# One weight product in the head of a convolution-and-attention kernel, by Strassen's rule

## Chip, cores and metric

The kernel runs on one NeuronCore of a Trainium2 chip. Times are device microseconds of one execution. Inputs and outputs are float32.

## What is computed

The reference has two layers. The first is an attention with deformed keys: a grouped 1x1 projection gives q, a depthwise convolution of q gives offsets, the input is sampled at the offset places, and a small network of positions (2 to 128 to 128 to 1) gives a bias for each of 1024 queries and 64 keys of each group. Softmax, output projection, and an MLP of 512 to 2048 to 512 follow. The second layer is a self-attention over the 1024 positions of each of two images. Cut to what matters:

```
bias = jax.nn.relu(bias @ cpb_w1 + cpb_b1)
bias = jax.nn.relu(bias @ cpb_w2 + cpb_b2)
bias = (bias @ cpb_w3 + cpb_b3).reshape(b, GROUPS, H * W, Hd * Wd)
sim = jnp.einsum('bhid,bhjd->bhij', qh, kh) + bias
...
q = xt @ Wq.T + bq
k = xt @ Wk.T + bk
v = xt @ Wv.T + bv
attn = jax.nn.softmax(jnp.einsum('bnc,bmc->bnm', q, k) / jnp.sqrt(jnp.float32(c)), axis=-1)
out = jnp.einsum('bnm,bmc->bnc', attn, v)
out = out @ Wp.T + bp
```

The kernel multiplies the weights of the second layer with each other beforehand: one 512x512 product joins Wq with Wk, and a second one joins Wv with Wp. The second product is the subject here.

## The kernel before

The work has four stages that follow each other.

*The head* (about the first 37 us). The offset chain of the first group runs: `chain(0)` projects q (L285), sums 36 taps of the depthwise convolution on VectorE (one L321 or L323 operation each, the two inputs being q in `qa` and the running sum `acc`), applies gelu on ScalarE (L355), multiplies on TensorE (L367), takes tanh (L377), and computes the positional values `fe` on VectorE and ScalarE by turns (L390 to L417). They are written to the DRAM tensor `fdr` (L418) and read back as `fb`, spread over all partitions (L599). From `fb`, ScalarE and VectorE make the tables `ta` and `tb` (L610, L616). Meanwhile `rank`, `order` and `arrange` sort the channels of the bias network by sign. They use small GpSimd operations (L233 to L235, and L260 to L266 for the scales `sc` and the small matrices `w3f` and `w3u`). TensorE fills its time with the two weight products `weights(0)` and `weights(1)`.

A weight product takes 16 matmuls of 128x128 weights by 512 columns into two PSUM tiles (L549), two ScalarE copies of 128x1024 into a half of the tile `gs` (L555), and one store to DRAM, `gdr[i]`, from GpSimd's queue (L557). `weights(1)` reads `wls[1]`, loaded by two transfers of 1 MB on the queue of SyncE (L537). The second layer reads both stored products back much later (`load_g`).

*The bias loop* (256 steps, most of the time). For each step s, `st_layer1` makes a tile `h1` of 128x4096 from `ta` and `tb` by one custom VectorE operation (L630; step 0 does it in two halves of 128x2048). `st_layer2` multiplies it in four parts z of eight matmuls (L647), each part into one of three PSUM tiles of the pool `zp`; ScalarE evicts each part (L656, L658), and VectorE adds them in pairs (L666, `st_sum`). Up to three `h1` tiles exist, in buffers of the tag `h1` that the two `wl_s` tiles and `gs` also use in the head. Steps 0 and 1 have small extra matmuls (`psu`, L515) behind them. Adding up the lanes of the sums is done by transfers.

*The projection and MLP*, and *the self-attention*, already use Strassen's rule for their large products. Its helpers stand at the top of the kernel:

```
PARTS = {1: (0, 0), 2: (1, 2), 3: (6, 3), 4: (2, 6), 5: (4, 4), 6: (5, 5), 7: (3, 1)}
FOLD = ((4, 3, 2), (5, 4, 0), (6, 5, 1), (3, 3, 0))
def fold(engine, w, sign=ALU.add, which=range(4)):
    for i in which:
        o, u, v = FOLD[i]
        engine.tensor_tensor(w[o], w[u], w[v], ALU.add if i % 2 else sign)
```

`fold` makes the four sums of one operand's blocks, `spread` (L125, L128) those of the other, always on VectorE. `PARTS` tells which block of each operand enters which of the seven products. `plus` (L137) is a VectorE sum.

Nothing sets the order of the work but the program: each engine runs its instructions in the order in which they are issued, which follows the program and a scheduler's estimate; `tc.issue_after(x)` gives an instruction a place behind x. The head's pieces are generators that are advanced by hand:

```
with tc.issue_after(newest(PE)):
    next(n)
for _ in n:
    pass
```

where `n` is the second product. Here its matmuls come behind those of `arrange` on TensorE.

Of the kernel before, what the change touches and what calls it, by code (L numbers as in the profile page):

```python
# [8 lines left out]
F32 = mybir.dt.float32  # L9
AF = mybir.ActivationFunctionType  # L10
ALU = mybir.AluOpType
# [3 lines left out]
P = 128  # L15
# [42 lines left out]
def conv_seq_kernel(ctx: ExitStack, tc: tile.TileContext, x, xt, kst, pst, cst, vec, wsm, outw, w1, w2, wl, wlt, brow, out):  # L58
    nc = tc.nc
# [4 lines left out]
    def newest(engine):  # L64
        return next(i for i in reversed(nc.cur_bb.bb.instructions) if i.engine == engine)
# [26 lines left out]
    gdr = [dp.tile([P, NCH, C], F32, name=f"gdr{i}") for i in range(2)]  # L92
    ub = cp.tile([P, 2, NCH], F32, name="ub")
# [18 lines left out]
    PARTS = {1: (0, 0), 2: (1, 2), 3: (6, 3), 4: (2, 6), 5: (4, 4), 6: (5, 5), 7: (3, 1)}  # L112
# [3 lines left out]
# [5 lines that stand above are left out]
    def spread(x, which=range(4)):  # L121
        for i in which:
            if i % 2 == 0:
                o, u = ((4, 0), (1, 3))[i // 2]
                nc.vector.tensor_tensor(x[o], x[u], x[1], ALU.subtract)  # L125
            else:
                o, u, v = ((5, 4, 3), (6, 5, 2))[i // 2]
                nc.vector.scalar_tensor_tensor(x[o], x[u], -1.0, x[v], ALU.mult, ALU.subtract)  # L128
# [7 lines left out]
    def plus(out, a, b_, op=ALU.add):  # L136
        nc.vector.tensor_tensor(out, a, b_, op)  # L137
# [8 lines left out]
    zp = ctx.enter_context(tc.tile_pool(name="zp", bufs=3, space=PSUM))  # L146
# [9 lines left out]
    with tc.tile_pool(name="lp", bufs=2) as lp:  # L156
# [80 lines left out]
        def order():  # L237
            nc.vector.tensor_scalar(k8, eight, rn[:, 1:2], 8.0, ALU.is_le, ALU.mult)
            nc.vector.tensor_reduce(t8, k8, AX.X, ALU.add)
            free, bound = ([t.rearrange("p (a b l) -> p b a l", a=2, b=2)[:, i] for t in (place, crow)] for i in (0, 1))  # L240
            nc.vector.tensor_scalar(bound[0], bound[1], t8, 64.0, ALU.is_ge, ALU.mult)
            nc.vector.tensor_tensor(bound[0], bound[0], bound[1], ALU.add)
            nc.vector.tensor_scalar(free[0], free[1], t8, None, ALU.add)
            nc.vector.tensor_scalar(perm, place, pc, None, ALU.is_equal)
# [26 lines left out]
        def chain(ci):  # L271
# [3 lines left out]
            for i in range(K):  # L275
                k = k0 + i
# [5 lines left out]
                ps = flat("psq")  # L282
# [76 lines left out]
            if ci == 0:  # L359
                ps = [simp.tile([P, 512], F32, name="sim") for _ in range(2)]  # L360
            else:
                ps = flat("po").rearrange("p (f m) -> p f m", f=2)
                ps = [ps[:, f] for f in range(2)]
# [24 lines left out]
            def place_keys(i0, i1):  # L388
                for i in range(i0, i1):
                    nc.vector.scalar_tensor_tensor(  # L390
                        th[:, i], th[:, i], 4.0, jg[:, i].unsqueeze(1).to_broadcast([P, 2 * K, J]),
                        ALU.mult, ALU.add,
                    )
                t = thf[:, i0 * n : i1 * n]
                nc.vector.tensor_scalar(t, t, 2.0 / 7.0, -1.0, ALU.mult, ALU.add)
# [4 lines left out]
            pos, ab, u, ln, er = (fe[0:64, i, :] for i in range(5))  # L400
# [5 lines left out]
            if ci > 0:  # L406
# [12 lines left out]
                out=fdr[ci].rearrange("g c p j -> p (g c) j"), in_=ab.rearrange("p (g j) -> p g j", j=KT)  # L419
            )  # L420
            if ci == 0:
                place_keys(0, 2)
            state[ci] = th
            yield
# [107 lines left out]
        wls = [lp.tile([P, 2, NCH, C], F32, tag="h1", name="wl_s", bufs=3) for _ in range(2)]  # L532
# [8 lines left out]
        gs = lp.tile([P, 2, NCH, C], F32, tag="h1", name="gs", bufs=3)  # L541

        def weights(i):
            ps = [flat("psg") for _ in range(2)]
            for o in range(NCH):
                for k in range(NCH):
                    if i == 0 and (o, k) in ((1, 0), (3, 1)):
                        yield
                    nc.tensor.matmul(  # L549
                        ps[k // 2][:, k % 2 * 512 : k % 2 * 512 + 512], wls[i][:, 0, o, k * P : (k + 1) * P],  # L550
                        wls[i][:, 1, o, :], start=(o == 0), stop=(o == NCH - 1),
                    )
            yield
            for k2 in range(2):
                nc.scalar.copy(gs[:, i, 2 * k2 : 2 * k2 + 2, :].rearrange("p k o -> p (k o)"), ps[k2])  # L555
            yield
            nc.gpsimd.dma_start(out=gdr[i], in_=gs[:, i])  # L557


        PE = mybir.EngineType.PE  # L560
        marks = []
        head, g, n = chain(0), weights(0), weights(1)
        next(head)
        next(g)
        with tc.issue_after(newest(PE)):
# [6 lines left out]
        with tc.issue_after(newest(PE)):  # L572
            next(g)
        order()
        for _ in head:
            pass
        with tc.issue_after(newest(mybir.EngineType.Activation)):
            next(g)
        with tc.issue_after(newest(PE)):
# [216 lines left out]
        for s in range(NS):  # L796
# [36 lines left out]
            if bg is None and s > ready and (s - ready) % 4 == 0 and (s - ready) // 4 <= 8:  # L833
                i = (s - ready) // 4 - 1
# [32 lines left out]
    uc = xq.tile([P, 2], F32, name="uc")  # L867
# [16 lines left out]
    with ExitStack() as top, tc.tile_pool(name="wp", bufs=2) as wp:  # L884
# [14 lines left out]
        for i, (b, h) in enumerate(halves):  # L899
            for o in range(NCH):  # L900
                n = slice(h * 512, (h + 1) * 512)
# [157 lines left out]
        for i, (b, p) in enumerate(units):  # L1059

            j, k = divmod(i, NCH)
# [324 lines left out]
```

## Time and profile before

| what | us |
|---|---|
| median of three runs | 2642.21 (2642.19 to 2644.27) |
| the profiled execution | 2641.35 |
| its span, first to last instruction | 2639.6 |
| TensorE busy | 2627.4 |
| VectorE busy | 2244.4 |
| ScalarE busy | 1693.6 |
| GpSimd busy | 783.6 |

The profile is that of one execution. A matmul of float32 stands in it as two records, so the 16 matmuls of a product are 32 records. PE is TensorE, PEld its weight loads, DVE VectorE, ACT ScalarE, POOL GpSimd, SP SyncE; L549 is line 549 of the kernel. A timeline row has its start and its length in us, the engine, the line, the operation, output and inputs, and in brackets how long the engine had been idle and what released it. In a view of groups, `| busy, mean ns | idle before` are totals and the mean of one. The shares of busy time are averages over the four stages; a change in the head is read from the head. The rows of the DMA view for the time from 26 to 28 us, and for that from 32 to 36 us, give each issue's size and the time to its landing:

```profile
gdr<-gs POOLq DMA_DIRECT2D x1, 1024.0 KB, 5.7
fb<-fdr SPq DMA_DIRECT2D x1, 512.0 KB, 5.7
```

```profile
fb<-fdr SPq DMA_DIRECT2D x1, 512.0 KB, 3.7
```

### The profile page before, as it was taken

How to read it: one execution, taken by the hardware profiler on the slowest of the kernel's cores; microseconds unless marked ns; L12 is line 12 of the kernel's file. 1: busy time of each engine (PE TensorE's matmuls, PEld its weight loads, DVE VectorE, ACT ScalarE, POOL GpSimd, SP SyncE). 2: the span in 40 equal slices, each digit the busy share in tenths (PEclk: the TensorE clock that was granted, in tenths of full speed). 3: DMA queues.
4: the chain of work that ended last, by engine and by line, in shares of the span. 5: the costliest groups of instructions: out<-in, count | busy, mean ns of one | idle time of the engine just before them, and what ended most of it. 6: DMA issues, size and time to landing. Idle time of an engine off the chain costs nothing.

```text
span 2639.6 us, 46955 instructions
## 1 busy us (share of the span) xinstructions
PE 2627.4 (100%) x19368; PEld 959.2 (36%) x19368; DVE 2244.4 (85%) x1333; ACT 1693.6 (64%) x2222; POOL 783.6 (30%) x863
## 2 busy tenths in 40 slices
PE   9999999999999999999999999999999999999999
PEld 3333322333333233333333333333344444446454
DVE  7999999999999999999999999999674494466354
ACT  5887898888888878887887777777621131114041
POOL 1333333333333333333333333333332232000000
PEclk9999999999999999999999999999999999999999
DMA  5788877888878888888887878788721111000000
GB/s 189 178 178 173 197 165 167 183 181 196 174 170 172 182 181 191 178 175 174 174 181 171 176 173 181 173 176 180 190 87 50 42 56 56 4 17 0 32 1 32
DMA packets 116294, 366.77 MB, mean 139 GB/s; under 512 B 23376, under 2 KB 27616, under 8 KB 113392
## 3 DMA queue, kind: packets, MB, share of 16 engines
q0 software_dynamic: 69408, 235.31, 47.5%
q1 hardware_dynamic: 46240, 128.15, 13.6%
q8 instruction: 153, 2.51, 0.4%
q14 instruction: 61, 0.50, 0.1%
q10 hardware_dynamic: 432, 0.31, 0.0%
HBM read 74.81 MB, written 6.55 MB: 31 GB/s over the span
## 4 chain that ended last, share of the span: by engine, by line
PE 93%; DVE 2%; ACT 2%; issue 2%; DMA 0%; DVEq 0%; ACTq 0%
PE ps L647 61%; PE sw L966 15%; PE sw L1101 9%; PE sw L913 2%; PE sw L1199 2%; PE sim L733 1%; DVE h L630 1%; PE psg L549 1%; ACT rx L656 0%; DVE ub L666 0%; ACT ub L658 0%; ACT prod L331 0%; PE pkv L483 0%; PE sim L716 0%; PE pt L750 0%
## 5 line engine op out<-in xcount | busy, mean ns | idle before, releaser
L647 PE MATMUL ps<-h,cw 128*32 128x512 f32 x16384 | 1777.2, 592 | 5.0 <-ACT rx L656 3.9
L630 DVE CUSTOM_DVE_ANT_1 h<-ta,tb 128x4096 f32<-128x4096 f32 (+1 forms) x257 | 1131.0, 4402 | 28.8 <-PE ps L647 25.8
L647 PEld LDWEIGHTS ps<-h,cw 128*32 128x32 f32 x16384 | 548.4, 110 | 1197.4 <-issue 1124.5
L656 ACT ACTIVATE rx<-ps,sc 128x1024 f32<-128x1024 f32 x512 | 567.8, 1109 | 145.7 <-PE ps L647 127.7
L658 ACT ACTIVATE ub<-ps,sc 128x1024 f32<-128x1024 f32 x256 | 308.0, 1203 | 93.7 <-PE ps L647 93.6
L666 DVE SCALAR_TENSOR_TENSOR ub<-rx,sc,ub 128x1024 f32<-128x1024 f32 x256 | 326.9, 1277 | 6.6 <-ACT ub L658 6.6
L685 POOL DMA_DIRECT2D ua<-uc x126 | 158.0, 1271 | 308.9 <-DMA ua<-uc 298.9
L685 POOL DMA_DIRECT2D ua<-ua x189 | 224.7, 1360 | 18.4 <-DMA ua<-uo 14.3
L966 PE MATMUL sw<-hm,w2t 128*128 128x512 f32 x448 | 193.6, 592 | 0.0
L966 PE MATMUL sw<-xb,w1t 128*128 128x512 f32 x448 | 193.6, 592 | 0.0
L668 POOL DMA_DIRECT2D uo<-ub x127 | 125.9, 991 | 222.7 <-DVE ub L666 207.0
L658 ACT ACTIVATE uo<-ps,sc 128x1024 f32<-128x1024 f32 x128 | 154.1, 1204 | 53.1 <-PE ps L647 52.7
L666 DVE SCALAR_TENSOR_TENSOR uo<-rx,sc,uo 128x1024 f32<-128x1024 f32 x128 | 163.6, 1278 | 9.4 <-ACT uo L658 9.2
L137 DVE TENSOR_TENSOR hm<-hm,sw 128x1024 f32<-128x1024 f32 x56 | 67.5, 1218 | 105.7 <-PE sw L966 105.5
L685 POOL DMA_DIRECT2D uc<-uo x63 | 53.6, 852 | 323.8 <-DMA uc<-uo 318.1
L975 ACT ACTIVATE hm<-hm,vs 128x512 f32<-128x512 f32 x64 | 42.5, 713 | 128.5 <-DVE hm L137 128.5
L966 PEld LDWEIGHTS sw<-hm,w2t 128*128 128x128 f32 x448 | 85.0, 190 | 107.5 <-issue 106.5
L966 PEld LDWEIGHTS sw<-xb,w1t 128*128 128x128 f32 x448 | 85.1, 190 | 107.1 <-issue 105.5
L137 DVE TENSOR_TENSOR xs<-xs,sw 128x1024 f32<-128x1024 f32 (+1 forms) x48 | 55.5, 1171 | 71.8 <-PE sw L1101 36.0
L668 POOL DMA_DIRECT2D ua<-ub x64 | 59.3, 927 | 174.1 <-DVE ub L666 166.6
L1101 PE MATMUL sw<-aT,vt 128*128 128x512 f32 x224 | 96.7, 593 | 0.3 <-ACT aT L1181 0.3
L610 ACT ACTIVATE ta<-fb,vs 128x512 f32<-128x512 f32 (+1 forms) x65 | 89.4, 1379 | 9.2 <-DMA fb<-fdr 9.2
(248 smaller groups left out, 2187.0 us busy)
## 6 DMA issues: line engine op xcount, KB each, us to landing
uo<-ub POOLq DMA_DIRECT2D x127, 512.0 KB, 5.5
fb<-fdr SPq DMA_DIRECT2D x64, 512.0 KB, 5.4
ua<-ub POOLq DMA_DIRECT2D x64, 512.0 KB, 5.6
uc<-ub POOLq DMA_DIRECT2D x64, 512.0 KB, 5.2
ua<-ua POOLq DMA_DIRECT2D x63, 256.0 KB, 6.2
ua<-uo SPq DMA_DIRECT2D x63, 256.0 KB, 2.4
ua<-uo POOLq DMA_DIRECT2D x63, 256.0 KB, 6.0
uc<-uc POOLq DMA_DIRECT2D x63, 256.0 KB, 6.9
```

The costliest lines, as they stand in the source:

```text
L137: nc.vector.tensor_tensor(out, a, b_, op)
L610: nc.scalar.activation(ta.rearrange("p j x -> p x j")[:, :, j0:j1], fb[:, 0, :, j0:j1], AF.Identity, bias=col("cb1"), scale=col("w1x"),)
L630: nc.vector._custom_dve(TENSOR_ADD_SAT, out=h1[:, y : y + step].rearrange("p y t x -> p (y t x)"), in0=a.unsqueeze(1).to_broadcast([P, ste ...
L647: nc.tensor.matmul(ps[32 * q : 32 * q + 32, h, :], cw2[:, 32 * z : 32 * z + 32], h1[:, 16 * h : 16 * h + 16, q, :], start=True, stop=True,)
L656: nc.scalar.activation(o, ps, AF.Relu, bias=sc[:, 4 + z : 5 + z])
L658: nc.scalar.activation(o, ps, AF.Relu, bias=sc[:, 4 + z : 5 + z], scale=sc[:, z : z + 1])
L666: nc.vector.scalar_tensor_tensor(r[1], r[0], sc[:, z : z + 1], r[1], ALU.mult, ALU.add)
L668: nc.gpsimd.dma_start(out=sums[s][1], in_=sums[s][3], accum_op=ALU.add)
L685: nc.gpsimd.dma_start(out=out, in_=in_, accum_op=ALU.add)
L913: nc.tensor.matmul(ps[:, m, :], w[a][:, k, m * P : (m + 1) * P], x[b_][:, k, :], start=(k == 0), stop=(k == 1),)
L966: nc.tensor.matmul(ps[:, m, :], w[:, a, k, m * P : (m + 1) * P], x[:, b_, k, :], start=(k == 0), stop=(k == 1),)
L1101: nc.tensor.matmul(ps[:, m, :], w[:, a, k, c + m * P : c + (m + 1) * P], x[b_][:, k, :], start=(k == 0), stop=(k == nk - 1),)
```

## The change

`weights(1)` is replaced by a new generator, `weights_n`. It cuts both 512x512 operands into four blocks of 256x256 and forms the product from seven products of such blocks. The sums of the first operand's blocks are made by GpSimd (`fold(nc.gpsimd, A)`), those of the second by VectorE (`spread(Bs)`); one sum of each is written over a block of the loaded weights, three of each into new tiles of the tags `ua` and `ub`. Each of the seven products is four matmuls of 256 columns (`form`) into a PSUM tile of the pool `zp`. The results are combined on the way out: three copies by ScalarE (parts 1, 3 and 5), six sums by VectorE, and one sum by GpSimd (part 6, into c12). The store to `gdr[1]` stays on GpSimd's queue.

The generator is advanced at other places. The folds of the first operand are issued behind `order()`. A second mark is recorded, VectorE's last operation before the write to `fdr` (L417), and the sums of the second operand are issued behind that mark. The products keep their place behind `arrange` on TensorE.

```diff
@@ chain(0)
             if ci == 0:
+                marks.append(newest(mybir.EngineType.DVE))
                 place_keys(0, 2)
@@ before the head is issued
+        def weights_n():
+            def spare(names):
+                return [lp.tile([P, 2, 512], F32, name=n, bufs=c)[:, :, 0:256] for n, c in names]
+
+            a, b_ = wls[1][:, 0], wls[1][:, 1]
+            A = [a[:, o : o + 2, k : k + 256] for o, k in ((0, 0), (2, 0), (2, 256), (0, 256))]
+            Bs = [b_[:, o : o + 2, c : c + 256] for o in (0, 2) for c in (0, 256)]
+            A += spare([("ua", 4)] * 3)
+            Bs += spare([("ub", 3)] * 3)
+            t, = spare([("uc", 2)])
+            fold(nc.gpsimd, A)
+            yield
+            c11, c12, c21, c22 = (gs[:, 1, k : k + 2, c : c + 256] for k in (0, 2) for c in (0, 256))
+
+            def form(ps, i, j):
+                for m in range(2):
+                    for o in range(2):
+                        nc.tensor.matmul(
+                            ps[:, m, 0:256], A[i][:, o, m * P : (m + 1) * P], Bs[j][:, o, :],
+                            start=(o == 0), stop=(o == 1),
+                        )
+
+            def less(out, u, v):
+                nc.vector.scalar_tensor_tensor(out, u, -1.0, v, ALU.mult, ALU.subtract)
+
+            def n5(ps):
+                nc.scalar.copy(c22, ps)
+                plus(c12, c12, ps)
+
+            def n6(ps):
+                plus(t, t, ps)
+                nc.gpsimd.tensor_tensor(c12, c12, t, ALU.add)
+
+            def n7(ps):
+                plus(t, t, ps)
+                less(c22, c22, t)
+
+            took = {
+                1: lambda ps: nc.scalar.copy(t, ps), 2: lambda ps: plus(c11, t, ps),
+                3: lambda ps: nc.scalar.copy(c12, ps), 6: n6, 5: n5, 7: n7, 4: lambda ps: less(c21, ps, t),
+            }
+            spread(Bs)
+            yield
+            for p in (1, 2, 3, 6, 5, 7, 4):
+                ps = zp.tile([P, 2, 512], F32, tag="ps2", name="sn")
+                form(ps, *PARTS[p])
+                took[p](ps[:, :, 0:256])
+            yield
+            nc.gpsimd.dma_start(out=gdr[1], in_=gs[:, 1])
+
         marks = []
-        head, g, n = chain(0), weights(0), weights(1)
+        head, g, n = chain(0), weights(0), weights_n()
@@ the head is issued
         order()
+        next(n)
         for _ in head:
             pass
+        with tc.issue_after(marks[1]):
+            next(n)
         with tc.issue_after(newest(mybir.EngineType.Activation)):
             next(g)
```

## The prediction

> **What bounds the kernel now.** I read the page's busy shares first, then the chain of waits for the first 60 us (the part that the change touches), then VectorE's timeline there, then the traffic. By the shares TensorE is never free, and between 60 and 1900 us it is busy for 1835.75 of 1840 us: whatever moves the start of that main loop moves the end by as much.
>
> ```profile
> PE 2627.4 (100%) x19368; PEld 959.2 (36%) x19368; DVE 2244.4 (85%) x1333; ACT 1693.6 (64%) x2222; POOL 783.6 (30%) x863
> ```
>
> The chain of waits (start, length, what) shows what sets that start:
>
> ```profile
> 23.55 13.93 PE psg L549 x32
> 37.48 3.62 PE ps L647 x32
> ...
> 41.18 1.20 ACT ua L658
> 42.38 1.27 ACT ta L610
> 43.65 0.46 ACT tb L618
> 44.11 0.46 ACT rx L656
> ...
> 45.01 1.20 ACT ub L658
> ...
> 46.25 7.12 PE ps L647 x64
> ```
>
> The second weight product (the 32 records from 23.55) ends at 37.48, where the first bias step begins. From its second eviction (41.18) a chain on ScalarE leads to the second step at 46.25. It looks as if a shorter product would start the loop sooner. VectorE's timeline (start, busy) says otherwise:
>
> ```profile
> 10.84 7.47 DVE L323 SCALAR_TENSOR_TENSOR acc<-qa,vs,acc 128x64 f32<-128x64 f32 x33
> ...
> 24.75 0.28 DVE L417 SCALAR_TENSOR_TENSOR fe<-fe 64x128 f32<-64x128 f32 x1
> 32.99 0.49 DVE L616 TENSOR_SCALAR tb<-fb,vs 128x512 f32<-128x512 f32 x1 [7.96 <-DMA fb<-fdr]
> 33.70 8.83 DVE L630 CUSTOM_DVE_ANT_1 h<-ta,tb 128x2048 f32<-128x2048 f32 x3 [0.22 <-ACT ta L610]
> 42.45 1.28 DVE L666 SCALAR_TENSOR_TENSOR ua<-rx,sc,ua 128x1024 f32<-128x1024 f32 x1
> ```
>
> 33 taps, a chain of small operations to 25.03, a transfer there and back (fb lands at 32.99, call this moment F), then h of step 0 in two halves of 2.289 us (group row of the 2048 form). The second starts at 33.70+2.21, so ends at 38.20 = F+5.21, and half of every bias matmul group needs it: TensorE's weight load of 38.24 is released by it. Two chains arrive together, and the change shortens only one.
>
> [...] in the MLP, where GpSimd does the same 128x512 sum (VectorE's timeline, then GpSimd's):
>
> ```profile
> 1974.30 1.21 DVE L137 TENSOR_TENSOR xs<-xs,sw 128x1024 f32<-128x1024 f32 x1
> 1975.43 1.22 DVE L128 SCALAR_TENSOR_TENSOR hm<-hm 128x1024 f32<-128x1024 f32 x1
> 1976.57 2.29 DVE L125 TENSOR_TENSOR hm<-hm 128x1024 f32<-128x1024 f32 x1
> 1978.78 2.28 DVE L128 SCALAR_TENSOR_TENSOR hm<-hm 128x1024 f32<-128x1024 f32 x1
> ```
>
> ```profile
> 1975.56 8.32 POOL L119 TENSOR_TENSOR w1t<-w1t 128x512 f32<-128x512 f32 x4 [10.61 <-DMA w1t<-in_w]
> ```
>
> 1.22 becomes 2.29: each fold holds VectorE 1.07 us, and four folds (1.268 us each alone, as in gg and gn) stretch from 5.05 to 8.32. [...] Here the wake matmuls start 0.85 us apart (2.41, 3.27, 4.12) and the products later 0.43 (8.04, 8.47); no run-time gap in the trace exceeds 1.23 us[...].
>
> **The change part by part**, in the order in which the changed program stands on each engine.
>
> 1. The product: 16 matmuls of 512 columns become 28 of 256, 7/8 of the columns: 13.93 x 7/8 = 12.19 us, 1.74 saved, so 1.74 us for each of seven parts. In front of h's second half this buys only that part of the next block is done early: one of eight matmuls, 7.0/32 = 0.22 us. Two ScalarE evictions of 1.01 us become three of half the size; ScalarE waits for TensorE there anyway. Nothing.
>
> 2. The four folds on GpSimd, behind the rank work (ends 13.6) and released by the first half of the weights: issued at 6.93, landed 7.5 us later, 14.43. At that moment 17 of the 33 taps are left ((18.22-14.43)/0.226), and a tap reads qa and acc, both in SBUF. Each fold gets in between two taps, as the one-element GpSimd operations at 11.85 and 12.49 did (0.53 and 0.69 us there, 0.22 for their like at 25.29), and holds the next for 1.07: 4 x 1.07 = 4.3, say 4.4 with the broken overlap of the taps. Bounds: 0 (taps always win) to 4 x 1.27 = 5.1. No gain is possible. No cover exists: gof, the offset matmuls, tanh, all to fdr and fb move by it. TensorE, whose nine psg matmuls ended at 19.37 with the L367 group next, stands for about 4.3 us; a half-rate start of that group (0.89 us) would cost up to 0.8: I take 0.2.
>
> 3. VectorE's four spread sums (0.684 each for 128x512) stand behind L417 and before fb lands, in an idle stretch of 7.96 us: hidden. But they hold GpSimd's small sc and w3 operations (25.29 to 26.8), and behind these waits the first gdr store, issued at 26.77. Four holds of up to 0.65, less the 0.3 pace that these have anyway, push it by about 1.7. [...]fb took 5.7 us beside it, while the next fb took 3.7 (traffic rows). So F comes earlier by between 0 and 2.0; I take 1.3.
>
> 4. The evictions on VectorE. Part 2's is early. Then the program's order is: tb, t of part 6, h's first half, c12 of part 5, t of part 7, h's second half, two more sums, h of step 1. All wait behind tb, hence behind F. With a pace of 0.62 and 0.683 each: t ends F+1.10; h's first half runs F+1.05 to F+3.34 (before: F+0.71 to F+3.00). GpSimd's sum into c12 needs that t, so it asks just after h's first half has begun; h reads ta and tb, two SBUF inputs, so GpSimd waits to F+3.34, ends F+4.60, and VectorE's c12, which needs it, ends F+5.33; t of part 7 at F+5.95; h's second half F+5.88 to F+8.17 instead of F+5.21: 2.96. If h doesn't exclude GpSimd (its custom operation never met one in the trace) it is 1.3 less. Queued behind: h of step 1 ends F+13.7, while TensorE needs it at F+16. The ScalarE chain of 5.1 us from the second eviction follows unchanged. With the 0.22 of point 1: +2.75.
>
> 5. h of step 2 now waits for step 0's matmuls, its buffer being that of step 0: it gets about 9 us before it is used. gdr[1] is read only at 2344. The main loop's order is otherwise the old one. A lag of VectorE against TensorE of 1.4 us disappears in VectorE's idle time (28 us in front of h over the loop). Nothing.
>
> Sum: 4.4 + 0.2 + 2.75 - 1.3 = +6.05 us. The profiled execution took 2641.35 us (span 2639.6), so 2647.4; the median of the runs, 2642.21, stands 0.86 higher, and I carry that over: 2648.3.
>
> **The rivals.**
> A. The taps aren't held: VectorE's short operations win, or GpSimd waits for the stream to end. For it: at 11.85 the taps kept their pace of 0.23 beside GpSimd. Against: those touched one element. 2.75 - 1.3 to 2.75: 2643.7 to 2645; point 2644.3.
> B. Heavier: fb isn't earlier, and TensorE, starved around F+3 to F+8 (busy some 3 of 5 us), starts the bias steps at half rate: z0 and z1, 2.4 us, take twice that. 4.4 + 0.8 + 2.75 + 2.4 = +10.3: 2652.5. [...]
> C. The other side, not slower: the exclusion doesn't act in the head and fb is the shared transfer that counts. Place: between fdr and tb. With F earlier by the full 2.0 and only the two evictions and the 0.35 of part 6 before h's second half (1.38), it is -0.6: 2641.6. It decides from the point where the folds hold the taps for less than 0.6 us in all. For it: both store and fb end together at 32.5.
> D. It doesn't do what it says: the last parts fall behind F, so the product isn't in the head's shadow. Its place is real: part 4's matmuls wait for the PSUM tile that part 6's t frees after F. TensorE then only trades one wait for another: about 2643 with A's other terms.
>
> **How the numbers follow.** A measurement of this kernel tells 0.2% (5.3 us, so 2647.5) from no change. My forecast 0.58 (its own range 2646 to 2650.5), A 0.14, B 0.15, C 0.10, D 0.03. Of the forecast's share about 0.42 lies above 2647.5; with B, slower 0.57. A part of C with an even shorter fb, faster 0.04; the rest, 0.39, no change. The range leaves out C's and D's lower part and B's tail: 2643.0 to 2653.0.
>
> **What would show it.** The taps' group longer than 7.47 by over 4 us, single taps of about 1.3 us, and GpSimd's folds stretched from 14.4 to over 20; a gap on TensorE after 19.4; the fb landing in under 5 us; GpSimd's c12 sum waiting through h's first half, and h's second half at F+8.2 with TensorE's step 0 waiting for it. I am wrong if the taps still end near 18.3, or if the second bias step begins less than 3 us after 46.25.

## The result, and the profile after

The changed kernel took 2651.53 us in the median of six runs (2649.27 to 2654.61), beside 2642.27 for the kernel before on the same chip (six runs, 2640.66 to 2644.27): 1.0037 times as long, with a 95% interval of 1.0027 to 1.0047. It is slower by about 9 us. Its profiled execution took 2650.11 us (span 2648.3), 8.76 us more than that of the kernel before.

Line numbers have moved with the 55 added lines: L647 is now L702, L630 is L685, L599 is L654, L616 is L671, and the second product is L580. The page's first part gives the shares again:

```profile
PE 2629.0 (99%) x19392; PEld 948.2 (36%) x19392; DVE 2252.7 (85%) x1343; ACT 1693.1 (64%) x2223; POOL 795.3 (30%) x868
```

TensorE's busy time is 1.6 us more, although the new product takes 1.6 us less of it. Six records of the first product (L550, 4.54 us, were 2.84) ran for the most part at half rate (granted clock 0.61 in the stretch from 24 to 26 us, 0.54 from 26 to 28), which is 1.7 us; the first bias step, now in two pieces, takes 1.0 us more (1.90 and 6.21 us, 7.07 before), and the matmuls of q (L285) take 0.6 us more. Where the time went is read from the timeline of the head (start, busy time, engine, line, operation; in brackets the idle time before it and what ended that):

```profile
11.09 11.62 DVE L323 SCALAR_TENSOR_TENSOR acc<-qa,vs,acc 128x64 f32<-128x64 f32 x33
15.20 1.27 POOL L119 TENSOR_TENSOR ua<-wl_s 128x512 f32<-128x512 f32 x1 [0.93 <-DMA wl_s<-in_wl]
...
19.17 1.30 POOL L119 TENSOR_TENSOR ua<-ua,wl_s 128x512 f32<-128x512 f32 x1
23.55 0.89 PE L367 MATMUL sim<-gof,ws 64*128 64x64 f32 x12 [3.71 <-ACT gof L355]
24.36 4.54 PE L550 MATMUL psg<-wl_s 128*128 128x512 f32 x6
...
29.30 0.70 SPq L418 DMA_DIRECT2D fdr<-fe  x1
32.30 18.67 SPq L654 DMA_DIRECT2D fb<-fdr  x3
32.53 0.66 POOL L558 DMA_DIRECT2D gdr<-gs  x1
36.77 0.49 DVE L671 TENSOR_SCALAR tb<-fb,vs 128x512 f32<-128x512 f32 x1 [2.83 <-DMA fb<-fdr]
...
37.77 2.29 DVE L685 CUSTOM_DVE_ANT_1 h<-ta,tb 128x2048 f32<-128x2048 f32 x1
37.99 3.19 POOL L594 TENSOR_TENSOR gs<-gs,uc 128x512 f32<-128x512 f32 x1 [4.43 <-DVE uc L137]
41.21 0.69 DVE L137 TENSOR_TENSOR gs<-gs,sn 128x512 f32<-128x512 f32 x1 [1.16 <-POOL gs L594]
42.42 2.28 DVE L685 CUSTOM_DVE_ANT_1 h<-ta,tb 128x2048 f32<-128x2048 f32 x1
```

The taps' group, 7.47 us before, is 11.62 us, and the four folds on GpSimd run exactly in it (15.20 to 20.47). TensorE waits 3.71 us for the gelu behind the taps. `fb` lands at 36.77 (F) instead of 32.99. Then VectorE's `c12` (41.21) waits for the sum on GpSimd, which in turn waited through the first half of h: it took 3.19 us where a fold takes 1.27. So h's second half ends at 44.70, F+7.93, instead of F+5.21. The chain of waits (start, length, what) shows that it now sets when TensorE can go on with the first bias step:

```profile
29.49 12.30 PE sn L580 x56
...
41.82 0.68 DVE uc L137
42.50 2.21 DVE h L685
...
44.75 5.87 PE ps L702 x52
...
52.77 7.12 PE ps L702 x64
```

The product took 12.30 us instead of 13.93, and ended at 41.79. The chain names this end as what released the sum at 41.82, but that sum also follows `c12` (41.21) by 0.61 us, the pace of VectorE in such a row; in the second profile of this kernel, further down, it does the same (44.16, then 44.77), 1.6 us after the product's end. TensorE then began the first bias step with ten records, stood until 44.75, and reached the second bias step at 52.77, 6.52 us later than the 46.25 of before. The remaining 2.2 us to the 8.76 were lost inside the loop, in pieces; the experiments come back to them.

### The profile page after: what moved, and what is told of

The parts are those of the page before. It is cut to its first block, busy times and chain, and to the rows that moved or that the text cites. A ratio compares the mean times of both kernels' runs of the same rounds, so it can differ in the third digit from the quotient of the medians.

```text
span 2648.3 us, 47025 instructions
## 1 busy us (share of the span) xinstructions
PE 2629.0 (99%) x19392; PEld 948.2 (36%) x19392; DVE 2252.7 (85%) x1343; ACT 1693.1 (64%) x2223; POOL 795.3 (30%) x868
## 4 chain that ended last, share of the span: by engine, by line
PE 84%; DVE 7%; issue 4%; ACT 2%; DMA 2%; DVEq 0%; POOL 0%; ACTq 0%; POOLq 0%; SPq 0%
PE ps L702 53%; PE sw L1021 15%; PE sw L1156 9%; DVE h L685 3%; PE sw L968 2%; PE sw L1254 2%; DVE ub L721 1%; PE sim L788 1%; ACT rx L711 1%; DVE uo L721 1%; PE sn L580 0%; DMA uc<-uo 0%; DMA ua<-uc 0%; DVE acc L323 0%; DMA xn<-in_x 0%
## 5 line engine op out<-in xcount | busy, mean ns | idle before, releaser
L702 PE MATMUL ps<-h,cw 128*32 128x512 f32 x16384 | 1778.0, 592 | 6.8 <-ACT rx L711 4.6
L685 DVE CUSTOM_DVE_ANT_1 h<-ta,tb 128x4096 f32<-128x4096 f32 (+1 forms) x257 | 1130.8, 4400 | 28.2 <-PE ps L702 25.8
L702 PEld LDWEIGHTS ps<-h,cw 128*32 128x32 f32 x16384 | 532.6, 110 | 1216.2 <-issue 1148.7
L119 POOL TENSOR_TENSOR w1t<-w1t 128x512 f32<-128x512 f32 x32 | 59.7, 1885 | 108.9 <-DMA w1t<-in_w 108.3
```

Of the source, the lines that this page charges most:

```text
L685: nc.vector._custom_dve(TENSOR_ADD_SAT, out=h1[:, y : y + step].rearrange("p y t x -> p (y t x)"), in0=a.unsqueeze(1).to_broadcast([P, ste ...
L702: nc.tensor.matmul(ps[32 * q : 32 * q + 32, h, :], cw2[:, 32 * z : 32 * z + 32], h1[:, 16 * h : 16 * h + 16, q, :], start=True, stop=True,)
```

## The experiments

The kernel before had medians of 2642.39, 2642.46, 2642.49, 2642.01 and 2641.86 us beside the five groups of runs. In the table, "second step" is the start of the second bias step in the profile against 46.25 of the kernel before; "loop" is what the profiled span then differs further from 2639.6 (end minus second step); "median" is the timed median against the median of the kernel before on the same chip. A single profile of each kernel stands behind the two columns in the middle.

| kernel | second step | loop | median | ratio, 95% interval |
|---|---|---|---|---|
| changed | +6.5 | +2.2 | +9.3 | 1.0037 (1.0027 to 1.0047) |
| changed, again | +9.5 | +1.7 | +10.1 | 1.0040 (1.0025 to 1.0055) |
| folds on VectorE | +0.7 | +5.2 | +4.5 | 1.0018 (1.0011 to 1.0025) |
| folds alone | +5.7 | +4.3 | +6.6 | 1.0026 (1.0015 to 1.0037) |
| no late sums | +5.0 | +1.2 | +5.7 | 1.0022 (1.0014 to 1.0031) |
| c12 on VectorE | +6.1 | +5.6 | +8.9 | 1.0034 (1.0024 to 1.0044) |
| before, again | -0.3 | +0.3 | | one run |
| store behind tables | +0.1 | +2.8 | | one run |
| delay alone | +0.9 | +2.0 | +1.9 | 1.0006 (0.9998 to 1.0015) |
| kept warm, 8 | +8.7 | +3.1 | +10.7 | 1.0035 (1.0021 to 1.0049) |
| kept warm, 4 | +5.1 | +1.1 | +5.6 | 1.0027 (1.0017 to 1.0037) |
| copies, then sums | +0.6 | +6.4 | +3.7 | 1.0014 (1.0006 to 1.0023) |
| parts in order | -0.4 | +1.7 | +0.2 | 1.0003 (0.9995 to 1.0011) |

**The folds moved from GpSimd to VectorE**, behind the last operation ahead of fb's transfer:

```diff
-            fold(nc.gpsimd, A)
             yield
...
+            fold(nc.vector, A)
             spread(Bs)
```

> The changed kernel, but the four folds of the first operand are made by VectorE, with the spread behind L417 where VectorE waits for fb. GpSimd holds no tap then. My theory: the 33 taps take 7.5 us again (11.6 in the changed kernel), TensorE has no gap after 19.4 and no half-rate stretch, fb lands near 32. In the order that this program has, the sum of part 6 stands between the two halves of h and the first bias matmuls wait for the PSUM tile of part 5, so the second bias step begins at F+17, near 49 us (52.8 in the changed kernel, 46.3 before): 2645 us. The rival that VectorE is the bound, so that its added busy time passes to the end as it is (8.3 us busy and 8.8 us longer in the two profiles): 2.7 us more of it, so 2654 us. The rival that the seven smaller products or the new order of the loop cost the time: no change from 2651.5.

Measured: 2646.85 us, 4.7 us less than the changed kernel, although VectorE has more to do. The taps are back at 7.46 us and TensorE has no gap in front of the offset matmuls. The timeline shows two more things:

```profile
25.01 4.64 POOL L260 TENSOR_SCALAR sc<-sc 128x1 f32<-128x1 f32 x1 [11.68 <-ACT sc L257]
27.02 18.09 SPq L654 DMA_DIRECT2D fb<-fdr  x3
30.39 0.52 DVE L671 TENSOR_SCALAR tb<-fb,vs 128x512 f32<-128x512 f32 x1
31.02 0.66 POOL L558 DMA_DIRECT2D gdr<-gs  x1
34.08 3.18 POOL L593 TENSOR_TENSOR gs<-gs,uc 128x512 f32<-128x512 f32 x1 [0.55 <-ACT gs L588]
```

GpSimd's one-column operation L260, 0.22 us before, took 4.64 us beside the row of VectorE sums. The first `gdr` store behind it was issued only after `fb` had landed, and `fb` took 3.37 us (27.02 to 30.39) instead of 5.69. So F came 2.6 us earlier than in the kernel before, which pays for most of the evictions' delay: the second step began at 46.91, only 0.66 us late (I had expected 49, with `fb` near 32). The end was nevertheless 5.9 us late in the profile.

**The folds alone**, added to the kernel before as four unused GpSimd sums of the same blocks; its second product and its loop are the old ones:

```diff
         order()
+        bl = [wls[1][:, 0][:, o : o + 2, k : k + 256] for o, k in ((0, 0), (2, 0), (2, 256), (0, 256))]
+        ex = [lp.tile([P, 2, 512], F32, name="ua", bufs=4)[:, :, 0:256] for _ in range(4)]
+        for out_, u_, v_ in ((ex[0], bl[3], bl[2]), (ex[1], ex[0], bl[0]), (ex[2], ex[1], bl[1]), (ex[3], bl[3], bl[0])):
+            nc.gpsimd.tensor_tensor(out_, u_, v_, ALU.add)
```

> The kernel before, with nothing but four GpSimd sums of 128x512 added where the changed kernel has its folds; they read the same weights, write to free tiles, and nothing reads them. My theory: they hold four taps for 1.1 us each, so the taps take 11.6 us instead of 7.5, fdr and fb come 4.2 us later, TensorE stands 3.7 us before the offset matmuls[...], which delays the product of 13.9 us to an end near 43.5. The second bias step begins near 52 us instead of 46.3: 2648 us. The rival that short VectorE operations are not held in any way that matters, or that the cost lies in the products and their sums: 46.3 us and 2642.3 us.

Measured: 2649.01 us. The timeline:

```profile
10.83 11.65 DVE L323 SCALAR_TENSOR_TENSOR acc<-qa,vs,acc 128x64 f32<-128x64 f32 x33
...
29.12 14.00 PE L549 MATMUL psg<-wl_s 128*128 128x512 f32 x32
51.91 4.50 PE L651 MATMUL ps<-h,cw 128*32 128x512 f32 x40 [0.43 <-ACT ub L662]
```

The taps take 11.65 us, as in the changed kernel, and the second step is 5.66 us late, as the old product too is pushed back to 29.12. Four GpSimd sums, 5.6 us together, that nobody reads cost the kernel 6.6 us. Together with the first experiment this settles the hold of the taps: it comes with the folds on GpSimd and goes with them.

**The second product left incomplete**: parts 6, 5, 7 and 4 are only copied out of PSUM by ScalarE and their combining sums are left out.

```diff
-                plus(c12, c12, ps)
...
-                plus(t, t, ps)
-                nc.gpsimd.tensor_tensor(c12, c12, t, ALU.add)
+                nc.scalar.copy(t, ps)
...
-                plus(t, t, ps)
-                less(c22, c22, t)
+                nc.scalar.copy(t, ps)
...
-                3: lambda ps: nc.scalar.copy(c12, ps), 6: n6, 5: n5, 7: n7, 4: lambda ps: less(c21, ps, t),
+                3: lambda ps: nc.scalar.copy(c12, ps), 6: n6, 5: n5, 7: n7, 4: lambda ps: nc.scalar.copy(c21, ps),
```

> The changed kernel without the sums that stand behind fb: parts 6, 5, 7 and 4 are only copied out of PSUM by ScalarE, and the four VectorE sums, the two subtractions and GpSimd's sum are left out, so that the second product is not complete. My theory: the taps stay at 11.6 us and fb stays late by 3.8, but h's second half follows the first at once and ends at F+5.2, near 42 us instead of 44.7; the second bias step begins near 50 us, 2.8 earlier than in the changed kernel: 2648.7 us. The rival that only GpSimd's folds count and these sums lie in slack: 52.8 us and 2651.5. The rival that VectorE's busy time is the bound: 4.1 us less of it, 2647.4 us, but then h's second half need not move.

Measured: 2648.06 us. The halves of h are one piece again, and end 5.1 us after F (37.23):

```profile
37.87 4.49 DVE L682 CUSTOM_DVE_ANT_1 h<-ta,tb 128x2048 f32<-128x2048 f32 x2 [0.15 <-ACT ta L662]
...
42.41 7.07 PE L699 MATMUL ps<-h,cw 128*32 128x512 f32 x64
51.26 4.93 PE L699 MATMUL ps<-h,cw 128*32 128x512 f32 x44 [0.43 <-ACT ub L710]
```

The second step begins 14.0 us after F, 2.0 us sooner than in the changed kernel, not the 2.7 us of the sums: the product, started late behind the held taps, ends no earlier than h now. The median is 3.5 us below the changed kernel's.

**Part 6's second sum on VectorE instead of GpSimd** (one line, `plus(c12, c12, t)` for the GpSimd sum):

> The changed kernel with part 6's second sum on VectorE instead of GpSimd. Theory of the prediction's step 4 (GpSimd's sum waits through h's first half and holds h's second half): without it h's second half ends near F+6.2 instead of F+7.9, the second bias step begins at about F+14.3, that is 1.7 us earlier than in the changed kernel, and the time is 1.7 us less. Rival (the loss is the place of the evictions behind tb, whichever engine sums: TensorE's first bias matmuls need the PSUM tiles that these evictions free after h's halves): h's second half ends earlier, but the first bias step still waits for the eviction of part 5 and the second begins within 0.5 us of F+16.0; the time is the same.

Measured: 2651.36 us, the time of the changed kernel. The timeline:

```profile
37.07 0.69 DVE L137 TENSOR_TENSOR uc<-uc,sn 128x512 f32<-128x512 f32 x1 [1.49 <-PE sn L580]
...
42.68 0.68 DVE L137 TENSOR_TENSOR gs<-gs,sn 128x512 f32<-128x512 f32 x1
43.41 7.07 PE L702 MATMUL ps<-h,cw 128*32 128x512 f32 x64 [1.20 <-DVE gs L137]
```

F was 35.10. h's second half ended at F+7.7 and the second step began at 52.30, F+17.2. That is later than either theory had it: `fb` landed 1.7 us sooner than in the changed kernel, while part 6, behind a clock at half rate for 6.8 us (0.93 in the stretch from 20 to 22 us, 0.50 from 22 to 28, 0.87 from 28 to 30), left TensorE no sooner. So part 6's eviction (37.07) waited for TensorE until F+2.0; in the changed kernel it began at F+0.4. Taking off these 1.6 us leaves F+15.6, an estimate, nearer to the rival's 16.0 than to the theory's 14.3. That speaks for the rival: GpSimd's wait is what the trace names, but the same sum put on VectorE seems to cost about the same, because the evictions still stand between tb and the second half, and TensorE waits for the PSUM tile of part 5 (43.41, behind the eviction at 42.68). It is not shown, for it rests on one profile and on a correction as large as the effect, and the medians cannot tell 1.7 us apart (the intervals of the two ratios overlap almost wholly). This edit together with the folds on VectorE, with which the clock stayed full above (1.00 in the first 60 us), was not run.

**The kernel before with the first gdr store behind the fb load:**

```diff
-            nc.gpsimd.dma_start(out=gdr[i], in_=gs[:, i])
+            (nc.gpsimd if i else nc.sync).dma_start(out=gdr[i], in_=gs[:, i])
...
         load_tables(0)
+        with tc.issue_after(newest(mybir.EngineType.SP)):
+            next(g, None)
```

> The kernel before with the first gdr store issued behind the fb load instead of 0.5 us ahead of it, and nothing else. Prediction's step 3[...]: fb lands 3.7 to 4.5 us after its issue instead of 5.69, so F moves from 32.99 to 31.0 to 31.8 and h's second half ends 1.2 to 2 us earlier; the second bias step stays within 0.4 us of 46.25, since the second product still ends at 37.48, and the time stays at 2642. Rival (fb's landing has other causes): F stays within 0.5 us of 33.0.

The timeline:

```profile
27.43 0.34 SPq L597 DMA_DIRECT2D fb<-fdr  x1
27.86 0.38 SPq L557 DMA_DIRECT2D gdr<-gs  x1
31.88 0.48 DVE L614 TENSOR_SCALAR tb<-fb,vs 128x512 f32<-128x512 f32 x1 [6.73 <-DMA fb<-fdr]
46.38 7.07 PE L645 MATMUL ps<-h,cw 128*32 128x512 f32 x64 [0.43 <-ACT ub L656]
```

`fb` took 4.45 us instead of 5.69, by the order of two transfers alone. As expected it moved nothing: the second step stayed at 46.38, since the product ended at 37.53. The one run took 2644.24 us, within the range of the kernel before.

**The changed kernel a second time**, to see how much its head varies:

> The changed kernel once more, for a second profile: does the part of the loss that came after the second bias step (2.2 us of 8.8 in the first profile, 1.7 of it one wait for a lane transfer near 611 us) come back at the same place? If it belongs to the change, TensorE waits there again and the loop from the second step to the end is 2.2 us longer than before again. If it is a matter of the single execution, the head's loss of 6.5 us is the same within 0.5 and the rest differs by a few us either way.

Measured: 2652.52 us, and in its profile a second step at 55.72, 3 us later than in the first. The timeline:

```profile
23.56 1.54 PE L367 MATMUL sim<-gof,ws 64*128 64x64 f32 x12 [3.89 <-ACT gof L355]
25.03 5.27 PE L550 MATMUL psg<-wl_s 128*128 128x512 f32 x6
...
29.97 0.70 SPq L418 DMA_DIRECT2D fdr<-fe  x1
33.51 0.66 POOL L558 DMA_DIRECT2D gdr<-gs  x1
34.03 19.88 SPq L654 DMA_DIRECT2D fb<-fdr  x3
39.72 0.49 DVE L671 TENSOR_SCALAR tb<-fb,vs 128x512 f32<-128x512 f32 x1 [4.39 <-DMA fb<-fdr]
```

The offset matmuls took 1.54 us instead of 0.89, the write of `fdr` 4.06 us until `fb` could be issued (29.97 to 34.03) instead of 3.00, and the store now went 0.5 us ahead of the load, so that `fb` took 5.69 us again. From F on everything is as in the first profile: the second step at F+16.0. The table by stretches of 2 us (busy times of the engines, then TensorE's granted clock, the transfers' share and GB/s) has the reason for the first of these, in the second profile (in the first profile of the changed kernel the clock stands at 0.61 and 0.54 between 24 and 28, which is 3.4 us):

```profile
22.00:24.00 2.00, 0.44 (x4) 0.44 (x6) 1.86 (x12) 0.35 (x1) 0.00 (x0) 0.78 0.00 0
24.00:26.00 2.00, 2.00 (x13) 1.41 (x12) 0.46 (x3) 0.85 (x3) 0.00 (x0) 0.50 0.01 4
26.00:28.00 2.00, 2.00 (x4) 0.92 (x3) 1.68 (x10) 1.93 (x6) 0.00 (x0) 0.50 0.00 0
28.00:30.00 2.00, 2.00 (x3) 0.77 (x3) 1.83 (x6) 0.98 (x2) 0.00 (x0) 0.51 0.00 0
```

The clock is at one half for 6.8 us (0.22 x 2 / 0.5 = 0.9, then 2.0, 2.0 and 1.96).

**The gap filled with idle matmuls**, eight of 128x512 and then four, between the first product's first part and the offset matmuls:

```diff
+        with tc.issue_after(newest(PE)):
+            wake(wls[0][:, 0, 0, :], *(512,) * 8)
         marks.append(newest(PE))
```

> The changed kernel with eight idle matmuls (128x512, into a spare PSUM tile) on TensorE between the first product's first part and the offset matmuls, that is in the gap of 3.7 us which the folds' hold opens. Theory (the gap lets the clock fall to half for 3.4 or 6.8 us, and this, not the sums, makes the head differ between the two profiles of the changed kernel): no stretch at half rate in the head, the offset matmuls near 0.65 us and the six records after them 2.84 us instead of 4.5 to 4.8; the second bias step at 52 to 53, and the time 1 to 2 us below the changed kernel's, near 2650. Rival (the half-rate stretch is hidden behind fb's wait and the spread of the head comes from the place of the gdr store against fb alone): the clock is full, but the second bias step and the time are the changed kernel's, 52.8 to 55.7 and 2651.5 to 2652.5.

> The changed kernel with four idle matmuls in the gap instead of eight: eight took 7.05 us (two records of 0.43 us each, not one) and so stood in front of the offset matmuls for 3.5 us after these were ready. Theory (the half-rate stretch costs the head up to 3 us in some executions): no half-rate stretch, the offset matmuls start near 23.4 and the records after them take 2.84 us; the second bias step begins at 52 to 52.8, and the time is 2649.5 to 2650.5, 1 to 2 us below the changed kernel. Rival (the stretch is hidden): full clock, second bias step 52.8 to 55.7, time 2651.5 to 2652.5.

With eight the clock stayed full (1.00 from 18 to 60 us), but they took 7.05 us and held the offset matmuls until 26.66: second step 54.92, time 2653.19 us. I had counted one record for a matmul of this size, and it is two. With four:

```profile
19.06 3.62 PE L162 MATMUL wake<-wl_s 128*32 128x512 f32 x8
23.89 2.84 PE L550 MATMUL psg<-wl_s 128*128 128x512 f32 x6
51.35 4.93 PE L704 MATMUL ps<-h,cw 128*32 128x512 f32 x44 [0.43 <-ACT ub L715]
```

The clock stays full (1.00 from 20 to 60 us), the six records take 2.84 us again, and the second step is at 51.35, 5.1 us late and again 16.0 us after F (35.39). The median of nine runs, 2647.56 us, is 4 us below the changed kernel's; the intervals of the two ratios still overlap (to 1.0037 here, from 1.0027 there), and single runs reach 2655.82. So the direction of the theory is supported, and its 1 to 2 us cannot be confirmed as a size. Of the 1.4 us between this profile and the first one of the changed kernel, 0.5 is an earlier start of the taps (10.59 against 11.09), and 0.8 a shorter write of `fdr` (2.24 us against 3.00), which no run explains.

**The loop's own losses.** All kernels with an edit lost time behind the second step; in the second profile of the changed kernel the loss (1.7 us) and a wait of 1.5 us at step 77 came back. Two runs ask whether the change makes it: the kernel before a second time, and the kernel before with its loop started a little later by three idle matmuls.

```diff
         for _ in n:
             pass
+        with tc.issue_after(newest(PE)):
+            wake(ident, 128, 128, 128)
```

> The kernel before, unchanged, profiled a second time. In the first profile the main loop lost nothing to its lane transfers; in each of the variants it lost 2 to 5 us between the second bias step and the end, at the same places (around steps 30, 39, 70 and 77 of 256). Theory L (the loss is made by the change of the head, which shifts the loop's transfers against each other): this profile again has the second bias step near 46.2 and ends within 1 us of 2639.6, with no wait of TensorE for a transfer near 600 us. Rival R (the loss comes and goes from one execution to the next, whatever the head does): about one chance in two that this profile shows such a wait, and a span of 2641 to 2645.

> The kernel before with three idle matmuls (128x128, six records of 0.11 us, some 0.65 us) on TensorE between the second product and the first bias step, and nothing else: the loop is the old one, started about 0.6 us later, as it was with the folds on VectorE (second bias step 46.91, time +4.5 us) and in the first rebuilt product (46.88, +3.7). Theory P (a shift of the loop's start alone brings out its losses at transfers): second step near 46.9, and the time 2645 to 2647, with losses near steps 70 to 78. Rival (the losses belong to what those kernels add on VectorE and in the buffers): second step near 46.9, and the time 2642.5 to 2643.5.

The kernel before ended at the same 2639.6 us, but not without a loss: its second profile waited once, and gained the time back later. The list of waits (engine and what it would do, what it waited for, us in total, times, longest) has 0.5 us for it (L733), for the first profile of the changed kernel:

```profile
PE sim L788 <- DMA ua<-uc: 1.7, 1, 1.7
```

and for the kernel with the delay alone:

```profile
PE sim L735 <- DMA ua<-uc: 1.9, 1, 1.9
```

Each stands at step 77 of 256, where the third layer of the bias network waits for a transfer between lanes. With the delay alone the second step was 0.85 us late and the profile's end 2.9; 2.1 us of that came between steps 70 and 77. The median, 2643.79, lies between what the two theories expected (2645 to 2647, 2642.5 to 2643.5). So a kernel that adds no sum, no buffer and no VectorE work can lose 2 us at that place; but that a shift of its start brings out the 3 to 4 us that stand in the medians of the two kernels with the same shift (folds on VectorE, copies then sums) is not shown. Part of the difference stands in the traces of these two kernels: step 77 cost them 4.1 and 3.9 us. TensorE waited there for 2.2 and 2.0 us, and its clock was lower. In the second of the two the weight loads show it: their groups start 0.75 to 0.86 us apart between 605.94 and 609.25, and 0.43 from there on, so four groups cost 1.6 us more. In the first the granted clock is 0.99 in the mean from 500 to 650 us, where the kernel before and the changed kernel have 1.00. With the delay alone TensorE waited for 1.9 us, and the granted clock was 1.0 in the mean of the execution. With c12 on VectorE it waited for 2.4 us; what the clock did there is not shown. In the other profiles it waited there for 1.7 us at most. What brings out the lower clock at this place stays open.

**The second product rebuilt**: all sums of the operands on VectorE in fb's transfer, the seven parts only copied to SBUF by ScalarE, and the sums of the result on VectorE, behind h's second half and behind h of step 1.

```diff
-            fold(nc.gpsimd, A)
+            x6, = spare([("uc", 2)])
+            x7, = spare([("uo", 3)])
...
+            took = dict(zip((1, 2, 7, 3, 6, 5, 4), (t, c11, x7, c12, x6, c22, c21)))
+            fold(nc.vector, A, which=(0,))
...
-                took[p](ps[:, :, 0:256])
+                nc.scalar.copy(took[p], ps[:, :, 0:256])
             yield
+            plus(c11, c11, t)
+            plus(t, t, x6)
+            plus(c12, c12, t)
+            plus(c12, c12, c22)
+            plus(t, t, x7)
+            less(c22, c22, t)
+            less(c21, c21, t)
```

> The second product by Strassen's rule, rebuilt: all eight sums of its operands on VectorE behind the last operation ahead of fb's transfer, the three parts that need none of them first (1, 2, 7, then 3, 6, 5, 4), each part only copied out of PSUM by ScalarE into SBUF, and the seven sums of the result on VectorE from SBUF, behind h's second half and behind h of step 1. My theory (what hurt was the hold of the taps and the evictions that stood between tb and h's second half): the taps take 7.5 us, TensorE has no gap, the product ends near 35.6, h's second half near 35.7, the first bias step begins near 36 and the second near 44.8, 1.4 us earlier than in the kernel before; the time 2640 to 2642, a gain of 0 to 1.5 us. Rival (any work added to VectorE in the head comes back in the loop, since VectorE is 97 per cent busy there): second step as above, but the loop loses 3 us or more as it did with the folds on VectorE, and the time is 2644 to 2646.

> The rebuilt second product again, with the parts in the changed kernel's order (1, 2, 3, 6, 5, 7, 4): part 7 reads two blocks that sums overwrite in place, so ahead of them it made TensorE wait 2.19 us for VectorE, and its copy stood ahead of the tables on ScalarE. Theory: TensorE has no gap in the product, which ends near 35.5; the tables start at fb's landing near 30.4, h's second half ends near 35.7, the first bias step begins at 35.6 to 36, the second near 44.7, 1.5 us earlier than in the kernel before. With a loop that loses nothing the time is 2641; with the loop's losses of the other rebuilt kernels (3 us) it is 2644. Rival (another wait takes the place): the second bias step no earlier than 46, the time 2645 or more.

The first took 2646.16 us. Part 7, put third, reads blocks that two sums overwrite in place, so TensorE waited 2.19 us for VectorE, and the first bias step began at 37.99, no earlier than behind the old product. Also, h waited 1.3 us for ScalarE's table, which this edit (not shown) puts behind part 7's copy. The second has the parts in the changed kernel's order (the order of the operand sums and the place of the tables follow, not shown):

```diff
-            took = dict(zip((1, 2, 7, 3, 6, 5, 4), (t, c11, x7, c12, x6, c22, c21)))
+            took = dict(zip((1, 2, 3, 6, 5, 7, 4), (t, c11, c12, x6, c22, x7, c21)))
```

Its timeline:

```profile
28.16 1.97 PE L581 MATMUL sn<-wl_s,ua 128*128 128x256 f32 x8 [0.99 <-DVE ua L119]
30.85 0.49 DVE L667 TENSOR_SCALAR tb<-fb,vs 128x512 f32<-128x512 f32 x1 [0.43 <-DMA fb<-fdr]
31.57 4.55 DVE L681 CUSTOM_DVE_ANT_1 h<-ta,tb 128x2048 f32<-128x2048 f32 x2 [0.23 <-ACT ta L661]
36.96 7.07 PE L698 MATMUL ps<-h,cw 128*32 128x512 f32 x64
45.84 7.07 PE L698 MATMUL ps<-h,cw 128*32 128x512 f32 x64 [0.43 <-ACT ub L709]
```

Now both chains in front of the loop are shorter: h's second half ends at 36.1 (38.20 before), the product at 37.03 (37.48 before). But TensorE waits 0.99 us for the folds, which cannot start before VectorE is free, and the second step is 0.4 us earlier, not 1.5. The time is 2642.71 us, not to be told from the kernel before. No version beat it.

## Why the prediction was right, step by step

The prediction was slower, 2648.3 us with a range to 2653.0; measured were 2651.53. The direction and most parts in the head were right, but the sum is 3.2 us short: the result lies above the forecast's own range (2646 to 2650.5), and inside the stated one by the room that this left upwards. Against the profile:

- *Step 1, the product* (12.19 us, worth 0.22): 12.30 us in the chain, right. The 0.22 was not gained: ten records of the first bias step were done early, but from the end of h's second half to the second step it was 8.07 us, and 8.05 before.
- *Step 2, the folds* (+4.4 for the taps): the group grew by 4.15 us, single taps took 1.33 to 1.35 us where a fold got in, and the `fdr` write was issued 4.24 us later. The two experiments with the folds settle the cause; rival A falls, and rival C too, whose bound was a hold of 0.6 us.
- *Step 2, the clock* (+0.2, an estimate for a gap that the trace of the kernel before does not have): mis-sized in its reach. The prediction priced the offset matmuls alone. TensorE's gap of 3.71 us came with half rate for 3.4 us and, in the second profile, that of 3.89 us with half rate for 6.8 us, and the six records behind them took 4.54 and 5.27 us instead of 2.84. Most of it was hidden behind the offset chain; what it put on the path was nothing in the first profile and 0.65 us in the second.
- *Step 3, the earlier fb* (-1.3): 4.47 us from issue to landing instead of 5.69, so -1.2. The experiment with the store shows the effect of the order of the two transfers, and the step's weak point is the second profile: the store slipped ahead of the load again, and the gain was gone.
- *Step 4, the evictions* (+2.75): from F to the second step 16.0 us in both profiles, 13.26 before: +2.74. That it fits to 0.01 is luck: h's second half ended at F+7.93, 0.24 sooner than the predicted F+8.17, and this made up for the 0.22 that step 1 did not bring. The order of events is the predicted one. Its cause, GpSimd's wait beside h, was an estimate from the sums of the MLP; the trace has it (3.19 us for the sum, 1.27 us alone). But the run with that sum on VectorE suggests that little is left of it as a cause; it does not settle it. That the delay belongs to the sums ahead of h's second half is shown twice: without them it ended at F+5.1, and in the last rebuilt kernel, where six of the seven sums stand behind it, at F+5.27 (36.12 with F at 30.85); before the change it was F+5.21. Neither run tells GpSimd's wait from the place of VectorE's own sums.
- *Step 5, the loop* (nothing): this failed. Of the 2.7 us by which the first profiled execution exceeds the predicted 2647.4, 0.5 came in the head (+6.52 for +6.05, as the `fdr` write took 0.76 us longer, for which there was no term) and 2.2 in the loop. VectorE's lag did disappear as stated, by step 13, but the loop waits for transfers at a few places with no reserve, and TensorE's share of 1835.75 of 1840 us, on which the step leaned, hid how near these are. The rest of the 3.2 us is that the median stands 1.4 above the profiled execution, not 0.86.

Rival B, heavier at 2652.5, came close in time. Its first half happened in the second profile (fb not earlier, half rate), but the half rate fell on the offset matmuls and the product's last six records, not on the bias steps. Rival D falls: the product's end was not what set the loop's start; in the second profile it came 1.7 us before TensorE began the first bias step, and the half rate that delays it left the 16.0 us behind F as they were. (Rival C's sum is off by 0.2 us: two evictions at the pace of 0.62 and the 0.35 of part 6 are 1.59, not 1.38.)

Why nothing could be won here is the other half: before the change, two chains met within a microsecond in front of the loop (the product at 37.48, h's second half at 38.20). Shortening one by 1.7 us was worth 0.2 us, an estimate; and the last rebuilt kernel, which shortens both, is held for 0.99 us by the wait for the folds on VectorE, wins 0.4 us in the head and loses 1.7 us in the loop of its profile.

## What to carry to other kernels

A sum moved to an engine that is idle was not free here: four GpSimd sums that nobody read, issued beside VectorE's chain of taps, cost 6.6 us. Ask of each eviction that a rewritten product adds where it stands in its engine's queue against the operation that the next stage waits for; on VectorE here sums of 0.68 us each, with GpSimd's between them, put h's second half 2.7 us behind its place. Where two chains end together, price a change by the later one, and where a long loop shows almost no waits, ask how much reserve its transfers have before calling its start the only thing that counts.

## What the runs showed of the hardware

- Beside VectorE's custom operation on two tiles in SBUF, GpSimd's 128x512 sum took 3.19 us in the changed kernel: it began 0.22 us behind h's first half (2.29 us) and ended 1.12 us behind that half's end. Alone such a sum takes 1.27 us (the groups `gg` and `gn` of the kernel before).
- Who gets in was not the same everywhere. Beside the taps a fold got in between two of them (1.35 us for the longest tap of the changed kernel, 0.32 before); beside the changed kernel's four spread sums GpSimd's small operations got in too (0.39 to 0.59 us for the first three in its first profile, 0.22 to 0.31 before). Beside a row of eight VectorE sums, 0.60 us apart, the first of them lasted as long as the row: 4.64 us with the folds on VectorE, and 5.24 us in both rebuilt kernels, where a ninth sum followed. What decides it no run shows.
- Gaps on TensorE in the head came with half rate. In the changed kernel a gap of 3.71 us came with 3.4 us of it, and the granted clock was 0.94 in the mean of the first 30 us; with the folds alone a gap of 3.66 us came with the same mean of 0.94. In the changed kernel's second profile and with c12 on VectorE, gaps of 3.89 and 3.90 us came with 6.8 us of half rate; in the second profile the mean of the first 30 us was 0.89, and it was 0.89 too in the kernel with no late sums (3.90 us). The kernel before, which has no such gap, has 1.00 there. With four idle matmuls in the gap the clock was 1.00 from 20 to 60 us. In the loops of two kernels waits of 2.0 and 2.2 us at step 77 went with a lower clock (the spacing of the weight loads in one, 0.99 in the mean from 500 to 650 us in the other). Waits of 1.9 us and less at the same step did not (1.9 us with the delay alone, 1.0 in the mean of the execution; 1.7 and 1.5 us in the two profiles of the changed kernel, 1.00 from 500 to 650 us). Nor did two waits at other places: 2.19 us in the head of the first rebuilt kernel (1.00 from 28 to 60 us), and 2.0 us in the loop of the kernel with the store behind the tables (1.0 in the mean of the execution). So the length of a wait alone does not decide it.
- The 512 KB load of `fb` took 3.4 to 3.6 us in the four profiles where the 1 MB store was issued 1.3 us behind it or later, 4.3 to 4.5 us in the five with the store 0.2 to 0.9 us behind, and 5.7 us in the three with the store 0.5 to 0.9 us ahead.
